# Layer norms of the first rows among the last attention products, shared row pools, and a start with eight adjacency loads

## The chip, the cores and the metric

The kernel runs on one core of one Trainium2 chip. A core has five engines that run side by side: TensorE (PE) for matrix products and transposes, VectorE (DVE), ScalarE (ACT), GpSimd (POOL), and SyncE (SP), which here only issues DMAs. Operands lie in SBUF, products land in PSUM. The metric is the device time of one launch in microseconds.

## The reference

The input is 4096 rows `x` of 256 features and a 4096 x 4096 adjacency of 0 and 1 with about 0.8% of ones and a full diagonal. Two graph attention layers come first, then one transformer layer:

```python
# twice: graph attention, 8 heads of 32 features
Wh = einsum('nd,hdo->hno', x, W)
e = leaky_relu(src[:, :, None] + dst[:, None, :], 0.2)     # src, dst = Wh . a
alpha = softmax(where(adj > 0, e, -9e15))
x = elu(einsum('hnm,hmo->nho', alpha, Wh)) + x
# once: transformer
q, k, v = split(layer_norm(x, g1, be1) @ w_qkv)
attn = softmax(where(adj != 0, q k^T * 32**-0.5, -inf))
x = x + (attn v) @ w_proj + b_proj
out = x + gelu(layer_norm(x, g2, be2) @ w1 + b1) @ w2 + b2
```

## The kernel before

**The two attention layers** are in `graph_attention`. The exponential of the leaky ReLU of a sum is one of two products of exponentials, depending on the sign of the sum. So the kernel needs per head only a 0/1 matrix that says where there is an edge and the sum is positive, the adjacency itself for all heads, and two sets of values weighted with exponentials. Sums over tokens are then products of 0/1 tiles with values, in f16 parts.

The work is cut into 256 *groups*: layer `l` (2), block `nb` of output rows (4 of 1024 rows), head pair `p` (4), and group `g` of four token tiles (8). Each group is 128 places of four products on PE (L1302), about 6 us. Beside its products every group carries a list `side` of steps for other engines, spread by a share of the group (`beside(steps, since, until)`). The steps are:

- `compare(i + 2)`: the 0/1 tile of the group after next. ACT makes one part of it (L1066), DVE another (L1068); one DVE instruction then puts the adjacency mask on (L1073). The comparison takes `s_b`, a broadcast of the terms of the rows, loaded through DRAM (`s_d`).
- `mask_load` (L855), `mask_clip` (L864, DVE: adjacency to fp8) and `mask_turn` (L886 PE transposes, L888 ACT copies): the adjacency, turned. The mask is kept in DRAM for the later head pairs, blocks and layers. The loads go into three `g_adj` buffers, the clips into six `adj_8` buffers.
- `preparation(l, q, bank)`: for one group `q` of four token tiles, the features are transposed (L961, L964), multiplied with the weights (L974), and the terms copied out (L981, DVE). ACT takes three exponentials of them (L987, L988), DVE the largest value (L989), the product of values and exponentials (L995, L1001). `split` makes two f16 halves: ACT casts the first (L1006), POOL subtracts (L1007). `term_rows` turns the terms (L1012, L1016) and stores them (L1019). Layer 1 has its first two preparations in `begin`, and six beside the first groups; layer 2 has eight beside the last groups of layer 1.
- `take`: a step of `pair_end` (L1101 to L1142), which closes a block and head pair on DVE, ACT and POOL, from copies of the PSUM banks that ACT makes (L1308, L1314).

The order on PE, ACT and DVE in `graph_attention` is that of the program text (a manual schedule over these three engines, which ends with the function). SP's order, and that of all engines in the transformer's first phase, is made by the scheduler.

`begin` loads the first rows and weights and three adjacency tiles, runs the preparations of `q` = 0 and 1, turns the first eight adjacency units (a unit is two row tiles of 1024 columns), and makes the comparisons of the first two groups.

**The transformer** (`unshifted_transformer`) opens with its QKV phase over eight blocks of 512 rows. `ready` loads the rows of a block and normalises them (`normed`: L1401 and L1402 mean, L1406 squares, L1410 root, L1414 normalised rows). `turned` transposes (L1430, PE) and copies with gamma and beta (L1433, ACT). Then come the products for k and q (L1502, copies L1506 ff) and v (L1521, L1528). Attention follows (L1554 to L1651), with the denominators' way over DRAM (`den_d` L1601, `u_dens` L1604, inverse L1608, L1609, `u_wide` L1614). The tail loads the weights (L1667 to L1679), and `projected` loads rows and attention (L742, L1692), projects (L1699, L1706) and normalises; the feed-forward follows (L1721, L1728, L1737, L1744, out L1745).

`Checks` collects conditions under which the fast path holds; otherwise a general path runs at the end.

Of the kernel before, what the change touches and what calls it, by code (L numbers as in the profile page):

```python
# [22 lines left out]
P = 128  # L23
# [727 lines left out]
def graph_attention(  # L751
# [6 lines left out]
    checks: Checks,  # L758
):

# [36 lines left out]
    stage_p = ctx.enter_context(tc.tile_pool(name="g_stage", bufs=2))  # L797
    rows_p = ctx.enter_context(tc.tile_pool(name="g_rows", bufs=2))
    t_p = ctx.enter_context(tc.tile_pool(name="g_t", bufs=3))
    s_p = ctx.enter_context(tc.tile_pool(name="g_s", bufs=2))  # L800
# [5 lines left out]
    ident_f = keep.tile([P, P], F32, name="g_ident_f")  # L806
    make_identity(nc, ident_f)
# [43 lines left out]
    def mask_load(nb, c, i):  # L851

        r = rows_p.tile([P, 2, G * P], I32, name="g_adj", bufs=3)
        at = STARTS[0][nb] * P + i * 2 * P
        nc.sync.dma_start(  # L855
            r,
            adj[at : at + 2 * P, c * G * P : (c + 1) * G * P].rearrange("(k r) m -> k r m", r=2),
        )
        loaded[nb, c, i] = r

    def mask_clip(nb, c, i):

        v = rows_p.tile([P, G * P, 2], F8, name="adj_8", bufs=6)
# [86 lines left out]
    def preparation(l, q, bank):  # L950
# [19 lines left out]
        def values(t):  # L970
# [10 lines left out]
            nc.vector.tensor_copy(  # L981
# [3 lines left out]
            big = some.tile([P, 2, H], F32, name="g_big")  # L985
            for i, scale in enumerate((-1.0, -LRELU)):
                nc.scalar.activation(big[:, i, :], L.negd[:, at, :], AF.Exp, scale=scale)  # L987
            nc.scalar.activation(L.r[:, at, :], L.terms[:, 0, at, :], AF.Exp, scale=LRELU - 1.0)  # L988
# [4 lines left out]
            prod = held[t] = some.tile([P, H, 2, V1], F32, name="g_prod")  # L993
# [9 lines left out]
        def split(t):  # L1003
            part = held.pop(t).rearrange("p h i v -> p h (i v)")
            halves = vst[q][:, t].rearrange("p h (k v) -> p h k v", k=2)
            nc.scalar.copy(halves[:, :, 0, :], part)  # L1006
            nc.gpsimd.tensor_tensor(halves[:, :, 1, :], part, halves[:, :, 0, :], op=ALU.subtract)  # L1007

        def term_rows():
# [5 lines left out]
            sr = some.tile([G * H, P], F32, name="g_sr")  # L1015
# [186 lines left out]
    def begin():  # L1202
# [3 lines left out]
        load_ahead(3)  # L1206
        units = own[: 2 * 2 * NW]
        for q in range(2):
            for k, step in enumerate(preparation(0, q, spare_bank)):
                step()  # L1210
                if q == 1 and k in (2, 4, 6, 8):
                    mask_clip(*units[k // 2 - 1])
        s_of[0, 0, 0] = s_fetch(0, 0, 0)
        for k, u in enumerate(units):
            mask_turn(*u)
            if k + 4 < len(units):
                mask_clip(*units[k + 4])
            else:
                mask_clip(*turns[0][k + 4 - len(units)])
# [8 lines left out]
    for i, (l, nb, p, g) in enumerate(groups):  # L1228
# [15 lines left out]
        if made:  # L1244
            steps = preparation(*made, lambda: turn_bank([P, 512], F32))
            beside(steps, 0.0, 0.9)
        if i + 2 < len(groups):
            steps = compare(i + 2)
            beside(steps[:-1], 0.25 if made else 0.0, 0.95)
            beside(steps[-1:], 0.96, 1.0)  # L1250
        beside([lambda u=u: mask_turn(*u) for u in turns.get(i, ())], 0.0, 0.9)
# [76 lines left out]

@with_exitstack
def unshifted_transformer(  # L1330
    ctx: ExitStack,
    tc: tile.TileContext,
    rows,
    mask_d,
    w_qkv: bass.AP,
# [3 lines left out]
    b1: bass.AP,  # L1339
    w2: bass.AP,  # L1340
    b2: bass.AP,
    g1: bass.AP,
    be1: bass.AP,
    g2: bass.AP,
    be2: bass.AP,
    out: bass.AP,
    checks: Checks,
):
# [30 lines left out]
    def by_feature(src, n, name):  # L1379
        t = wts.tile([P, n], F32, name=name)  # L1380
        with nc.allow_non_contiguous_dma(reason="one small vector"):
            nc.sync.dma_start(t, src.rearrange("(c p) -> p c", p=P))
        return t

    g1_sb = by_feature(g1, DC, "u_g1")
    be1_sb = by_feature(be1, DC, "u_be1")
    g2_sb = by_feature(g2, DC, "u_g2")
    be2_sb = by_feature(be2, DC, "u_be2")
    b1_sb = by_feature(b1, FC, "u_b1")
    ones = wts.tile([P, O], F32, name="u_ones")  # L1390
    nc.vector.memset(ones, 1.0)
    eps = wts.tile([P, 1], F32, name="u_eps")
    nc.vector.memset(eps, LN_EPS)
    ident_f = wts.tile([P, P], F32, name="u_ident")
    make_identity(nc, ident_f)
    dens = wts.tile([P, NQ, QI], F32, name="u_dens")

    def normed(xs, ln):

# [432 lines left out]
```

## Time and profile before

Three runs: 3472.72 to 3482.42 us, median 3479.99. The profiled execution has a span of 3480.2 us, with a mean granted PE clock of 0.983.

| stage | from to us | PE busy us | DVE busy us | ACT busy us |
|---|---|---|---|---|
| first loads and preparations | 0 to 62 | 19.05 | 31.73 | 24.56 |
| groups with preparation, layer 1 | 62 to 160 | 77.56 | 80.16 | 66.72 |
| groups, adjacency still loading | 160 to 380 | 211.32 | 210.31 | 198.26 |
| groups with preparation, layer 2 (part) | 880 to 985 | 86.10 | 83.98 | 74.49 |
| groups of layer 2 | 1034 to 1699 | 661.50 | 607.76 | 586.15 |
| its last eight groups | 1699 to 1746 | 46.69 | 36.23 | 34.44 |
| last pair, first norms | 1746 to 1763 | 4.73 | 13.24 | 12.74 |
| most of the QKV phase | 1763 to 1870 | 95.24 | 37.40 | 53.40 |
| end of attention, first projection | 3183 to 3220 | 15.49 | 8.87 | 7.30 |
| feed-forward | 3220 to 3480 | 251.50 | 42.15 | 85.70 |

Busy time is the time in which the engine works on an instruction; it may be less than the stage's length because the engine waits. A stage whose PE column equals its length is bound by PE. The stages of `graph_attention` have three busy engines and one order for each, so a wait in one soon becomes a wait in another.

### The profile page before, as it was taken

The page shows a single profiled execution, that of the slowest core. Times are in us where ns is not written, and L with a number is a line of the kernel's source. Part 1 is how long each engine was busy: PE and PEld are TensorE (multiplying, and loading weights), DVE is VectorE, ACT ScalarE, POOL GpSimd, SP SyncE. Part 2 cuts the span into 40 slices and gives each one's busy share as a digit, 9 for nine tenths or more (in the row PEclk, how much of TensorE's full clock was granted, in tenths as well). Part 3 has the DMA queues.
Part 4 walks back from the last instruction along what each step waited for, and adds up shares of the span by engine and source line. Part 5 has one row for each costly group of instructions (what it writes and reads, how often), then busy time and mean ns, then how long its engine had stood idle before and what let it go on. Part 6 is the DMA issues. An engine that isn't in the chain of part 4 may idle for free.

```text
span 3480.2 us, 97728 instructions
## 1 busy us (share of the span) xinstructions
PE 3297.8 (95%) x43156; PEld 2098.1 (60%) x43156; DVE 2880.6 (83%) x3250; ACT 2655.5 (76%) x3381; POOL 1323.4 (38%) x602
## 2 busy tenths in 40 slices
PE   4899999999889999999988999999999999997999
PEld 3799999999789999999953111111111111112666
DVE  6899999999779999999945999999999999996111
ACT  4799899988778888888855777777777777775332
POOL 1300000000210000000003999999999999996110
PEclk7999999999999999999989999999999999998999
DMA  6666555421311212121064010101011010002110
GB/s 203 190 181 205 154 154 164 139 84 27 96 51 39 72 48 87 39 75 39 12 178 113 19 31 19 32 25 25 25 26 37 13 44 10 26 10 67 44 47 26
DMA packets 214721, 250.57 MB, mean 72 GB/s; under 512 B 88528, under 2 KB 135632, under 8 KB 214288
## 3 DMA queue, kind: packets, MB, share of 16 engines
q1 hardware_dynamic: 214288, 244.25, 23.6%
q8 instruction: 339, 5.55, 0.7%
q14 instruction: 94, 0.77, 0.1%
HBM read 201.73 MB, written 42.47 MB: 70 GB/s over the span
## 4 chain that ended last, share of the span: by engine, by line
PE 39%; DVE 7%; ACT 4%; POOL 2%; issue 1%; DMA 1%; SPq 0%; DVEq 0%; ACTq 0%; POOLq 0%
PE u_ps L1554 12%; PE u_av L1568 11%; PE u_dn L1568 6%; DVE u_e L1563 4%; PE misc L1737 3%; PE bank L1302 2%; POOL u_both L1651 2%; PE misc L1502 2%; ACT u_ps L1561 1%; PE misc L1721 1%; PE misc L1521 1%; ACT ln_square L1406 1%; PE misc L1430 1%; DVE t L1073 1%; ACT t L1066 1%
## 5 line engine op out<-in xcount | busy, mean ns | idle before, releaser
L1302 PE MATMUL bank<-vst,t 128*128 128x66 f16 (+1 forms) x24576 | 1524.2, 203 | 47.5 <-DVE t L1073 39.6
L1302 PEld LDWEIGHTS <-t 128*128 128x128 fp8e4 x24576 | 1506.1, 97 | 66.5 <-DVE t L1073 47.9
L1302 PE MATMUL bank<-vst,mask 128*128 128x132 f16 x8192 | 1506.3, 222 | 0.0
L1066 ACT ACTIVATE t<-s_b,g_terms 128x1024 int8<-128x1024 f32 x1151 | 1243.6, 1165 | 98.6 <-PE bank L1302 94.7
L1651 POOL TENSOR_TENSOR u_both<-u_e 128x1024 f32<-128x1024 f32 x512 | 1200.1, 2368 | 232.6 <-DMA u_k<-half_d 126.1
L1563 DVE SCALAR_TENSOR_TENSOR u_e<-u_mask,u_ps 128x1024 f32<-128x1024 uint8 x1024 | 1201.7, 1215 | 89.2 <-ACT u_ps L1561 84.1
L1561 ACT ACTIVATE u_ps<-u_ps 128x1024 f32<-128x1024 f32 x1024 | 1010.8, 1008 | 281.4 <-PE u_ps L1554 262.4
L1302 PEld LDWEIGHTS <-mask 128*128 128x128 fp8e4 x8192 | 803.4, 98 | 0.0
L1073 DVE TENSOR_TENSOR t<-t,mask 128x2048 int32<-128x2048 int32 x256 | 589.8, 2304 | 111.0 <-ACT t L1066 89.6
L1068 DVE TENSOR_SCALAR t<-s_b,g_terms 128x1024 fp8e4<-128x1024 f32 x897 | 636.2, 753 | 0.0
L1554 PE MATMUL u_ps<-u_q,u_k 128*128 128x512 f16 x2048 | 579.1, 384 | 17.8 <-DVE u_e L1563 17.2
L1554 PEld LDWEIGHTS <-u_k 128*128 128x128 f16 x2048 | 139.0, 97 | 723.6 <-issue 664.6
L1568 PE MATMUL u_av<-u_e,u_v 128*32 128x512 f32 x4096 | 547.2, 606 | 0.0
L1007 POOL TENSOR_TENSOR vst<-g_prod,vst 128x528 f16<-128x528 f32 x64 | 83.9, 1321 | 938.5 <-ACT vst L1006 915.6
masks.py:197 POOL MEMSET u_ident<- 128x128 f32 x1 | 0.2, 205 | 727.5 <-ACT ln_square L1406 727.5
L1568 PE MATMUL u_dn<-u_both,u_ones 128*32 128x512 f32 x2048 | 274.0, 605 | 1.3 <-POOL u_both L1651 1.3
L1568 PEld LDWEIGHTS u_av<-u_e,u_v 128*32 128x32 f32 x4096 | 81.0, 108 | 219.2 <-issue 210.5
L1728 ACT ACTIVATE u_hid<-misc,u_b 128x512 f32<-128x512 f32 x64 | 42.3, 683 | 142.6 <-PE misc L1721 142.5
L1744 DVE TENSOR_TENSOR u_xres<-u_xres,misc 128x256 f32<-128x256 f32 x32 | 13.5, 421 | 122.7 <-PE misc L1737 122.7
L1737 PE MATMUL misc<-u_w,u_hid 128*128 128x256 f32 x512 | 111.8, 379 | 0.0
L1721 PE MATMUL misc<-ln_cols,u_w 128*128 128x512 f32 x256 | 111.2, 592 | 0.0
L864 DVE TENSOR_SCALAR adj<-g_adj 128x1024 fp8e4<-128x1024 int32 x128 | 97.1, 760 | 15.7 <-DMA g_adj<-in_adj_dram 15.7
(120 smaller groups left out, 1633.2 us busy)
## 6 DMA issues: line engine op xcount, KB each, us to landing
g_adj<-in_adj_dram SPq DMA_DIRECT2D x128, 512.0 KB
mask<-mask SPq DMA_DIRECT2D x128, 256.0 KB
s_b<-s_d SPq DMA_DIRECT2D x64, 512.0 KB
u_mask<-mask SPq DMA_DIRECT2D x32, 512.0 KB
mask<-stage SPq DMA_DIRECT2D x48, 256.0 KB
rows<-e_x SPq DMA_DIRECT2D x32, 256.0 KB
half_d<-u_halves SPq DMA_DIRECT2D x32, 256.0 KB
u_k<-half_d SPq DMA_DIRECT2D x32, 256.0 KB
```

The lines of the kernel that those rows point to most:

```text
L864: nc.vector.tensor_scalar(v.rearrange("p m r -> p r m"), loaded.pop((nb, c, i)), 1.0, -(2.0**-30), op0=ALU.min, op1=ALU.max, saturate=False,)
L1066: nc.scalar.activation(to.bitcast(I8), s, AF.Sign, bias=negd, scale=-1.0)
L1068: nc.vector.tensor_scalar(to, s, negd, None, op0=ALU.is_ge, saturate=False)
L1073: nc.vector.tensor_tensor(both, both, m32.unsqueeze(1).to_broadcast(list(both.shape)), op=ALU.bitwise_and)
L1302: nc.tensor.matmul(to, left, right, start=k not in opened, stop=last)
L1554: nc.tensor.matmul(ps[:, j, :], k_st[:, h, mt * P : (mt + 1) * P], q_st[:, h, :], start=True, stop=True,)
L1561: nc.scalar.activation(ps, ps, AF.Exp, scale=SCALE)
L1563: nc.vector.scalar_tensor_tensor(e, mask, 0.0, ps, op0=ALU.not_equal, op1=ALU.mult)
L1568: nc.tensor.matmul(to[j * O : (j + 1) * O, :], lefts[j], es[j // 2][:, j % 2, :], start=start, stop=stop,)
L1651: nc.gpsimd.tensor_tensor(both, es_of[i - 1][u], es_of[i][u], op=ALU.add)
L1721: nc.tensor.matmul(ph, w1_sb[:, k, f * P : (f + 1) * P], hn[:, k, :], start=(k == 0), stop=(k == DC - 1),)
L1737: nc.tensor.matmul(po[:, :D], hid[:, f, at : at + P], w2_sb[:, f, :], start=(f == 0), stop=(f == FC - 1),)
```

## The change

1. **Norms.** `normed` and `turned` become methods of a class `Norms`, made at the kernel's start with the small vectors (five small loads, now first on SP's queue), one f32 identity and a pool of small tiles. A class `Ahead` holds the rows, weights and columns of the QKV phase in buffers of the attention layers: `w_qkv` in `g_adj` slots, rows in `g_rows` slots, columns in `g_ft` slots. Its `steps` for row blocks 0 and 1 are handed into the last eight groups of layer 2: loads in group 0, means in 1, squares in 2, both roots in 3, normalised rows in 5 and 6, transposes and copies of block 0 in 7. The weights' loads have no wait on the groups; SP's order has them right after the last adjacency load. In the QKV phase each iteration turns the next block, normalises the one after, and loads the one after that at its end.
2. **Pools.** `stage_p` and `rows_p` are made outside of both functions, at the other side of SBUF (`side="right"`), and closed after the QKV phase. `adj_8` has five buffers instead of six, `g_sr` one, `g_big` four.
3. **Start.** The first eight adjacency loads are issued at once, three into `g_adj`, four into "mask" slots and one into a "t8" slot. Four clips stand beside the first preparation, turns and four more clips beside the second.
4. **Preparation.** The terms' copy goes from DVE to ACT, the exponentials read PSUM directly, layer 1's products lie in one wide tile (`ev_broad`'s slot), and the first half of `split` goes from ACT to DVE, except in `begin`. `check_values` (three reductions and three comparisons), which nothing called before, is called once per layer.
5. **Tail.** The projection's weight is loaded again there, and rows and attention of block 0 are loaded ahead of `b2`, `w1` and `w2`.

```diff
-        v = rows_p.tile([P, G * P, 2], F8, name="adj_8", bufs=6)
+        v = rows_p.tile([P, G * P, 2], F8, name="adj_8", bufs=5)
...
-            nc.vector.tensor_copy(
+            nc.scalar.copy(
                 L.terms[:, :, at, :], pv[:, D : D + 2 * H].rearrange("p (k h) -> p k h", k=2)
             )
-            big = some.tile([P, 2, H], F32, name="g_big")
+            big = some.tile([P, 2, H], F32, name="g_big", bufs=4)
             for i, scale in enumerate((-1.0, -LRELU)):
-                nc.scalar.activation(big[:, i, :], L.negd[:, at, :], AF.Exp, scale=scale)
-            nc.scalar.activation(L.r[:, at, :], L.terms[:, 0, at, :], AF.Exp, scale=LRELU - 1.0)
+                nc.scalar.activation(big[:, i, :], pv[:, D + H : D + 2 * H], AF.Exp, scale=scale)
+            nc.scalar.activation(L.r[:, at, :], pv[:, D : D + H], AF.Exp, scale=LRELU - 1.0)
...
-            prod = held[t] = some.tile([P, H, 2, V1], F32, name="g_prod")
+            if l == 0:
+                if t == 0:
+                    held["prods"] = ep.tile([P, G, H, 2, V1], F32, name="ev_broad")
+                prod = held[t] = held["prods"][:, t]
+            else:
+                prod = held[t] = some.tile([P, H, 2, V1], F32, name="g_prod")
...
-            nc.scalar.copy(halves[:, :, 0, :], part)
+            if first:
+                nc.scalar.copy(halves[:, :, 0, :], part)
+            else:
+                nc.vector.tensor_copy(halves[:, :, 0, :], part)
             nc.gpsimd.tensor_tensor(halves[:, :, 1, :], part, halves[:, :, 0, :], op=ALU.subtract)
...
-        load_ahead(3)
+
         units = own[: 2 * 2 * NW]
+        del coming[: len(units)]
+        for k, u in enumerate(units):
+            place = None
+            if 3 <= k < 7:
+                place = mask_p.tile([P, 2, G * P], I32, name="mask")
+            elif k == 7:
+                place = t_p.tile([P, 2, G * P], I32, name="t8")
+            mask_load(*u, place)
         for q in range(2):
-            for k, step in enumerate(preparation(0, q, spare_bank)):
+            for k, step in enumerate(preparation(0, q, spare_bank, True)):
                 step()
+                if q == 0 and k in (3, 5, 7, 9):
+                    mask_clip(*units[(k - 3) // 2])
                 if q == 1 and k in (2, 4, 6, 8):
-                    mask_clip(*units[k // 2 - 1])
+                    mask_turn(*units[k // 2 - 1])
+                    mask_clip(*units[k // 2 + 3])
         s_of[0, 0, 0] = s_fetch(0, 0, 0)
-        for k, u in enumerate(units):
-            mask_turn(*u)
-            if k + 4 < len(units):
-                mask_clip(*units[k + 4])
-            else:
-                mask_clip(*turns[0][k + 4 - len(units)])
+        for k in range(4, len(units)):
+            mask_turn(*units[k])
+            mask_clip(*turns[0][k - 4])
...
             steps = preparation(*made, lambda: turn_bank([P, 512], F32))
+            if made[1] == NG - 1:
+                steps.append(lambda: check_values(made[0]))
             beside(steps, 0.0, 0.9)
...
+        if i >= len(groups) - NG:
+            mine = [step for at, step in handed if at == g]
+            beside([lambda step=step: step(lambda: turn_bank([P, HB], F32)) for step in mine], 0.0, 0.9)
...
+    def steps(self):
...
+        all_ = [(0, self.weights)]
+        for at, step in ((0, self.load), (1, mean), (2, squares)):
+            all_ += [(at, lambda bank, nb=nb, step=step: step(nb)) for nb in range(2)]
+        all_.append((3, lambda bank: roots()))
+        all_ += [(5 + nb, lambda bank, nb=nb: self.normed(nb)) for nb in range(2)]
+        all_ += [(7, lambda bank, c=c: self.turned(0, c, bank())) for c in range(self.D // P)]
+        return all_
...
-            standing = {nb: ready(nb) for nb in range(2)}
-            across = turned(standing.pop(0), g1_sb, be1_sb, lnc, ps_q)
+            wq_sb = ahead.w
+            ahead.load(2)
             for nb in range(NNB):
                 cols = slice(nb * NB, (nb + 1) * NB)
-                hn = across
-                if nb + 2 < NNB:
-                    standing[nb + 2] = ready(nb + 2)
-                if nb + 1 < NNB:
-                    across = turned(standing.pop(nb + 1), g1_sb, be1_sb, lnc, ps_q)
+                hn = ahead.hn.pop(nb)
+                if nb + 1 < NNB:
+                    for c in range(DC):
+                        ahead.turned(nb + 1, c, ps_q.tile([P, NB], F32, name="misc"))
+                if nb + 2 < NNB:
+                    ahead.moments(nb + 2)
+                    ahead.normed(nb + 2)
...
                     nc.scalar.copy(v_sb[:, nb * TB + t, :], pv[:, :D])
+                if nb + 3 < NNB:
+                    ahead.load(nb + 3)
...
+        pools.close()
...
         bp_sb = by_row(b_proj, "u_bp")
-        b2_sb = by_row(b2, "u_b2")
-        w1_sb = big.tile([P, DC, F], F32, name="u_w1")
-        nc.sync.dma_start(w1_sb, w1.rearrange("(c p) f -> p c f", p=P))
-        w2_sb = big.tile([P, FC, D], F32, name="u_w2")
-        nc.sync.dma_start(w2_sb, w2.rearrange("(c p) e -> p c e", p=P))
+        wp_sb = big.tile([P, DC, D], F32, name="u_wp")
+        nc.sync.dma_start(wp_sb, w_proj.rearrange("(c p) e -> p c e", p=P))
...
+        first = rows_of(0)
+        b2_sb = by_row(b2, "u_b2")
+        w1_sb = big.tile([P, DC, F], F32, name="u_w1")
+        nc.sync.dma_start(w1_sb, w1.rearrange("(c p) f -> p c f", p=P))
+        w2_sb = big.tile([P, FC, D], F32, name="u_w2")
+        nc.sync.dma_start(w2_sb, w2.rearrange("(c p) e -> p c e", p=P))
...
+        stage_p = pools.enter_context(tc.tile_pool(name="g_stage", bufs=2, side="right"))
+        rows_p = pools.enter_context(tc.tile_pool(name="g_rows", bufs=2, side="right"))
+        ahead = Ahead(nc, norms, rows[2], stage_p, rows_p, w_qkv)
```

## The prediction, before the result was known

> **What bounds the kernel now.** I read the page first (busy time, slices, chain of waits), then busy time by stretch, then waits and timeline wherever TensorE falls below full.
>
> ```profile
> PE 3297.8 (95%) x43156; PEld 2098.1 (60%) x43156; DVE 2880.6 (83%) x3250; ACT 2655.5 (76%) x3381; POOL 1323.4 (38%) x602
> PE   4899999999889999999988999999999999997999
> PEclk7999999999999999999989999999999999998999
> ...
> PE 39%; DVE 7%; ACT 4%; POOL 2%; issue 1%; DMA 1%; SPq 0%; DVEq 0%; ACTq 0%; POOLq 0%
> ```
>
> TensorE is the bound: 182 us of 3480.2 are not PE. The slices show where a change can win: the first two (87 us each), the two eights at slices 11 and 12 (preparation of layer 2), the two at 21 and 22 (the passage from layer 2 to the transformer), and the 7 near the end. By stretch:
>
> ```profile
> 40.00:62.00 22.00, 0.61 (x4) 0.34 (x4) 8.76 (x11) 9.58 (x10) 0.00 (x0) 0.50 0.92 307
> 62.00:160.00 98.00, 77.56 (x1022) 66.70 (x1023) 80.16 (x149) 66.72 (x162) 30.42 (x23) 0.96 0.55 171
> ...
> 880.00:985.00 105.00, 86.10 (x1273) 76.15 (x1271) 83.98 (x158) 74.49 (x169) 31.07 (x24) 0.98 0.27 86
> 1034.00:1699.00 665.00, 661.50 (x14429) 657.33 (x14427) 607.76 (x690) 586.15 (x697) 0.00 (x0) 1.00 0.18 53
> 1699.00:1746.00 47.00, 46.69 (x1024) 46.39 (x1022) 36.23 (x41) 34.44 (x44) 0.00 (x0) 1.00 0.06 14
> 1746.00:1763.00 17.00, 4.73 (x22) 3.53 (x20) 13.24 (x31) 12.74 (x30) 0.61 (x2) 0.59 0.69 204
> ```
>
> Columns after the length: busy PE, weight loads, DVE, ACT, POOL, then clock, DMA share, GB/s. At 40 to 62 everything waits on DMA at 0.92; at 62 to 160 and 880 to 985 no engine is full (PE 79% and 82%, DVE 82% and 80%), so there the waits decide; the last eight groups of layer 2 (1699 to 1746) have a full PE with 10.8 us of DVE and 12.6 of ACT to spare; 1746 to 1763 is a PE hole.
>
> Waits from 62 to 160, then single places in the timeline (start, length, engine, line, idle before and its releaser):
>
> ```profile
> ACT g_big L987 <- DVE g_terms L981: 26.6, 24, 2.7
> PE turn L974 <- DVE g_prod L1001: 11.6, 12, 1.2
> DVE g_prod L995 <- POOL vst L1007: 4.6, 6, 0.8
> ```
> ```profile
> 55.93 0.70 DVE L864 TENSOR_SCALAR adj<-g_adj 128x1024 fp8e4<-128x1024 int32 x1 [2.23 <-DMA g_adj<-in_adj_dram]
> 1701.94 13.67 ACT L1066 ACTIVATE t<-s_b,g_terms 128x1024 int8<-128x1024 f32 x13
> 1754.80 2.09 PE L1430 MATMUL misc<-u_ident,ln_rows 128*128 128x128 f32 x8 [8.57 <-DVE ln_rows L1414]
> 1760.58 2.19 PE L1430 MATMUL misc<-u_ident,ln_rows 128*128 128x128 f32 x8 [3.69 <-DVE ln_rows L1414]
> 1812.29 2.19 PE L1430 MATMUL misc<-u_ident,ln_rows 128*128 128x128 f32 x8 [3.92 <-DVE ln_rows L1414]
> 3186.97 1.25 SPq L1601 DMA_DIRECT2D den_d<-u_den  x4
> 3192.99 0.35 SPq L1604 DMA_DIRECT2D u_dens<-den_d  x1
> 3193.86 0.51 SPq L1692 DMA_DIRECT2D u_att<-att_d  x1
> 3198.92 5.73 PE L1699 MATMUL misc<-u_wp,u_att 128*128 128x256 f32 x16 [12.94 <-DMA u_att<-att_d]
> ```
>
> **What the Trainium skill says.** "TensorE: Matmul & The Clock Gate", "What's actually happening": an idle window of about 3.4 us halves the array's clock. The trace agrees: eight transposes take 2.09 to 2.19 us after these idles and 1.04 in the stream, and the first block's QKV products 8.77 us against 7.03 later. So a hole of PE costs more than its length. "SBUF — State Buffer", "Who interferes with whom": VectorE and GpSimd share a port pair that one holds for a whole instruction. The trace agrees: a clip (L864) takes 0.69 us alone and 1.65 beside POOL's L1007. "VectorE: DVE Perf Modes", "Mode 2×_2P — use both read ports for one tensor": a one-source copy inside SBUF may run at two results per cycle. The trace has no such DVE copy here; L1139, one source, 512 elements of f32 in SBUF, takes 0.42 us and two-source L1140 0.69. I use those as the two ends for the new split copy.
>
> **Part 1, the start.** First products now begin at 62.3 us. The chain back: mask L1073 at 60.04 (2.29), five compares from 56.54, the clip at 55.93, which waited for an adjacency load; the clips waited 15.7 us in all on such loads, while the loads themselves were issued late, behind clips that free slots. The change issues eight loads (4.2 MB) at once from about 5.3 us, so at the measured 307 GB/s they are there by about 20 us. Against it: five small loads come first on SP (five issues of 0.45 us, +2.3), the second token group's rows are queued behind the 4.2 MB (arrival 20 to 25 us instead of before 19.3), so preparation q=1 ends near 35 instead of 33; and in SP's order three of the four s_d row stores stand behind loads that wait for clips of units 8 to 11, so the broadcast s_b is issued at about 43 (39.1 before) and lands at about 48.5 (47.40 before). Eight ACT compares then take 8.4 us beside DVE's, and the mask follows: first products at about 56. Gain 6, from 0 (s_b later than 54) to 10.
>
> **Part 2, the 14 preparation groups** (6 in layer 1, 8 in layer 2). Removed from DVE: four terms copies, 0.09 each start to start, 0.36 a group. Added: four split copies of 528, 0.42 to 0.70 each, 1.7 to 2.8 a group, perhaps more when POOL's subtract (1.15 to 1.4 us) holds the port. ACT loses four casts (0.62 each, 0.52 start to start) and gains four small copies of about 0.15: minus 1.5. The hop from DVE to ACT ahead of the exponentials (26.6 us over 24 tokens, 1.1 each) goes, as they read PSUM; in layer 1 the single wide tile removes L995's wait on POOL (4.6 us over 6 groups, 0.76 a group). PE's wait for L1001 (11.6 over 6 groups, 1.9 each) shortens by what of the hop lies on it. DVE now has 98.0 − 80.2 = 17.8 us to spare over these 6 groups, 3.0 each, so +1.3 to +2.4 fits, just. I take +0.5 us a group gained in layer 1 (3 in all; ends −5 and +9), and 0 in layer 2, where the two-buffer wait stays (ends −8 and +6). One `adj_8` buffer less costs nothing: each clip starts at least 3.68 us after the transposes of the unit five before it. The value checks, three reductions and three comparisons once per layer, come to about 1.2 us of DVE a layer by L1685, whose reduction of 256 elements takes 0.42; −1 in all (0 to −2.5).
>
> **Part 3, norms in the last eight groups.** Added to ACT: eight squares with their accumulator reads (0.63 each, 5.1), two root sets (0.5) with two table loads of 1.28, two copies of 0.6: 9.4 of 12.6 spare. To DVE: two means (1.24 + 0.16) and two sets of four normalisations (1.5): 5.8 of 10.8 spare. To PE: eight transposes, 1.04, in full. The spare time of ACT is not spread evenly: 13 compares stand back to back from 1701.94 to 1715.6, and squares fall in the third group; the masks lead PE by only 1.4 to 1.9 us. A stall of about 1.5 us there is likely (0 to 6). So layer 2's last product ends at about 1746.2 + 2.5. The DMAs: two row loads and nothing of w_qkv, which goes into adjacency slots right behind the last adjacency load in layer 1; the DMA share is 0.06 there, so they are hidden.
>
> **Part 4, the passage.** Now from 1746.2 to the first QKV product at 1762.56: 16.4 us. After: ev copies free the banks, PE does the eight transposes of block 1 (1.0; block 0's are in part 3) and goes on to the QKV products of block 0, with its columns and weights in place. Left are about 1.5 us. Gain 16.4 − 1.5 − 1.0 of the transposes + 1.4 of the clock (8.77 against 7.03, most of it) = 15.3; minus the 2.5 above: 12.8, say 12 (7 to 15). The last pair's finish on DVE (L1101 to L1141, about 10 us) runs beside QKV products now, ahead of block 2's norm, which PE needs only after the 14 us of two blocks.
>
> **Part 5, QKV phase.** The holes before the transposes of blocks 5, 6 and 7 (3.92 each plus a slow clock) come from squares that ACT reaches after the copies of its iteration. That order stands in the new text. The last ones move by a microsecond either way: 0 to −1; I take −1.
>
> **Part 6, the tail.** PE waits 12.94 us for `u_att`, whose issue stands behind den_d's landing (5.11 us, behind the w1 and w2 loads) and u_dens. After, the first att load is ahead of b2, w1 and w2, issued near 3188.7, landing 4.9 later at most; den_d lands about 2.5 us sooner without w1 and w2 ahead of it. L1699 can then start near 3193 to 3195 and its chain moves with it, but the division's own part at 3196 stays for later blocks. Gain 5 (2 to 7). A second wp load is 0.26 MB, hidden.
>
> **Sum.** 6 + 3 + 0 − 1 + 12 − 1 + 5 = 24. Against the profiled span of 3480.2, which is the median of the other runs (3479.99): **3456 us**.
>
> **Rivals.** About 0.3%, 10.4 us, is what a measurement of this kernel can tell from no change: under 3469.6 is faster, over 3490.4 slower.
> - A, the sum above, 3447 to 3465: 0.55.
> - B, the hop was the limit of the preparation groups: PE loses 98 − 77.6 = 20.4 us in layer 1's six and 18.9 over 105 in layer 2. If of the 3.4 a group of layer 1 that makes 1.4 comes back in all 14, it is 20 instead of 3: about 3439. For it: 26.6 us of ACT waiting; against: DVE gets fuller. 0.20.
> - C, given back: the start stands still because s_b, and not the adjacency, ends the wait last (6 lost), and ACT's crowded last groups stall PE by 6 instead of 1.5 (5 lost), preparation gains nothing (3): about 3470. For it: s_b is issued behind more. 0.19, two thirds of it inside 0.3%.
> - D, slower: DVE becomes the bound of the 14 groups. The place is the split copy against POOL's subtract of the token before: at 0.70 plus a wait of up to 1.15 each, four cost 7.4, less 0.36 and 3.0 spare: 4 us a group, 56 in all, less the 21 that the other parts give: about 3515. It decides from (21 + 10.4)/14 = 2.2 us a group. Against it: copies and subtracts follow each other by token in any case, and POOL is idle 70%. 0.06.
>
> That it doesn't do what it says is not likely: the transposes of block 0 stand among the products in PE's order.
>
> **Numbers.** Faster 0.55 + 0.20 + 0.06 = 0.81, same 0.13, slower 0.06. The range 3438 to 3474 leaves out D, the outer part of B and the edge of C; A alone is 3447 to 3465.
>
> **What would show it.** First products near 56; no wait of g_big on g_terms, and the period of preparation groups at 15.8 instead of 16.3; PE whole to 1749 and the first L1502-like product within 3 us of it; L1699's twin starting near 3194. Wrong it is if DVE's compares or masks become PE's releaser in the preparation groups, if PE stands in the last eight groups for over 5 us, or if s_b lands after 54.

## The result and the profile after

The changed kernel takes 3461.38 us (median of 4 runs, 3457.66 to 3466.94) against 3480.85 (3472.72 to 3482.42) of the kernel before: ratio 0.995, 95% interval 0.9929 to 0.9971, so 19.5 us less. Its profiled run is the slowest of the four (3466.94, span 3465.2); the profiled pair differs by 15.0 us.

The page of the changed kernel: busy time, two rows of the slices, the chain of waits by engine.

```profile
PE 3293.5 (95%) x43156; PEld 2098.3 (61%) x43156; DVE 2899.7 (84%) x3254; ACT 2629.4 (76%) x3391; POOL 1328.6 (38%) x600
PE   4899999999889999999988999999999999998999
PEclk8999999999999999999999999999999999998999
PE 40%; DVE 7%; ACT 3%; POOL 2%; DMA 1%; issue 1%; SPq 0%; DVEq 0%; ACTq 0%; POOLq 0%
```

The slices hide the change: PE gains a tenth in one slice near the end, and its clock one in the first slice and one where the layers hand over to the transformer; it is busy 4 us less for the same instructions. DVE gained 19 us of work, ACT lost 26. What tells is the start of each group's first product and of each stage's first one, in both traces. (A group is 32 places of four products, 128 in all, and not 128 places. "Groups 0 to 9" is the time from the first product of group 0 to that of group 9.)

| stretch | before us | after us | gain us | forecast us |
|---|---|---|---|---|
| start to group 0 | 62.39 | 60.15 | +2.2 | +6 |
| groups 0 to 9, layer 1's preparations | 116.73 | 108.89 | +7.8 | +3 |
| groups 120 to 136, layer 2's preparations | 165.74 | 169.32 | −3.6 | −1, the checks in it |
| group 168 | 5.84 | 9.43 | −3.6 | none |
| last eight groups | 47.12 | 51.60 | −4.5 | −2.5 |
| last product to first QKV product | 16.56 | 2.25 | +14.3 | +13.9 |
| first QKV product to first of attention | 109.18 | 112.19 | −3.0 | +0.4 (1.4 clock, −1) |
| last score product to first of the feed-forward | 40.48 | 35.83 | +4.7 | +5 |

The rest (groups between, attention, feed-forward) adds 0.7 and makes 15.0. Of layer 2's 3.6 us, 1.0 is in group 131, which varies between runs. By stretch of the changed kernel, with the columns of before (PE, weight loads, DVE, ACT, POOL, clock, DMA share, GB/s):

```profile
40.00:60.00 20.00, 0.00 (x0) 0.00 (x0) 6.40 (x7) 5.46 (x6) 0.00 (x0) 0.50 0.70 227
60.00:151.00 91.00, 76.51 (x1027) 65.29 (x1028) 85.13 (x148) 59.57 (x167) 31.75 (x23) 0.98 0.60 181
873.00:1028.00 155.00, 130.37 (x1937) 118.17 (x1935) 133.56 (x223) 91.06 (x230) 47.28 (x32) 0.93 0.24 74
1697.00:1749.00 52.00, 48.36 (x1004) 48.04 (x1001) 42.88 (x56) 42.57 (x68) 0.00 (x0) 0.97 0.09 23
```

In layer 1's preparations DVE is now busy 94% of the time and ACT 65% (82% and 68% before), and still it is shorter: the waits, not the busy time, had set it. Waits from 58 to 160 us:

```profile
ACT g_terms L984 <- PE turn L977: 26.5, 24, 1.8
PE turn L977 <- DVE ev_broad L1009: 6.0, 10, 0.7
```

ACT still waits 26 us, but for PE and no longer for DVE; PE's wait for the products fell from 11.6 to 6.0 us.

The start, in the timeline: the broadcast's first issue in the kernel before, then SP's issues, a clip and ACT's comparisons in the changed one:

```profile
39.14 0.82 SPq L1049 DMA_DIRECT2D s_b<-s_d  x2
37.52 7.32 SPq L858 DMA_DIRECT2D g_adj<-in_adj_dram  x4
44.90 1.16 SPq L1030 DMA_DIRECT2D s_d<-g_sr  x3
49.15 1.74 SPq L1060 DMA_DIRECT2D s_b<-s_d  x4
43.58 0.70 DVE L867 TENSOR_SCALAR adj<-g_adj 128x1024 fp8e4<-128x1024 int32 x1 [3.93 <-DMA g_adj<-in_adj_dram]
54.54 8.42 ACT L1077 ACTIVATE t<-s_b,g_terms 128x1024 int8<-128x1024 f32 x8 [15.32 <-DMA s_b<-s_d]
```

The first eight adjacency tiles are clipped by 36.9, but three of the four stores of the terms stand behind four later adjacency loads. The last of these needs a buffer that a clip frees at 44.28, and this clip itself stood 3.93 us for a tile. So the broadcast of the terms is issued at 49.15 instead of 39.14, and ACT waits 15.3 us for it.

The passage, one of the QKV phase's holes, and the tail:

```profile
1748.03 1.09 PE L1412 MATMUL misc<-ident,g_rows 128*128 128x128 f32 x8 [1.10 <-ACT ev_narrow L1338]
1748.95 7.03 PE L1579 MATMUL misc<-g_ft,g_adj 128*128 128x512 f32 x16
1800.23 2.18 PE L1412 MATMUL misc<-ident,g_rows 128*128 128x128 f32 x8 [7.20 <-DVE g_rows L1399]
3177.09 0.47 SPq L1768 DMA_DIRECT2D u_att<-att_d  x1
3181.12 6.56 PE L1779 MATMUL misc<-u_wp,u_att 128*128 128x256 f32 x16 [6.39 <-DMA u_att<-att_d]
3194.05 3.11 DVE L1399 TENSOR_SCALAR ln_rows<-u_xres,n_mean,n_dev 128x256 f32<-128x256 f32 x4
```

PE stands 1.10 us where it stood 8.57 and 3.69, and the products that follow take 7.03 us from the first block on, where the first block took 8.77. The hole before block 5 grew from 3.92 to 7.20. In the tail PE waits 6.39 us for `u_att` instead of 12.94; but the normalisation that follows takes 3.11 us instead of 1.38.

### The profile page after: what moved, and what is told of

The parts are those of the page before. It is cut to its first block, busy times and chain, and to the rows that moved or that the text cites. A ratio compares the mean times of both kernels' runs of the same rounds, so it can differ in the third digit from the quotient of the medians.

```text
span 3465.2 us, 97706 instructions
## 1 busy us (share of the span) xinstructions
PE 3293.5 (95%) x43156; PEld 2098.3 (61%) x43156; DVE 2899.7 (84%) x3254; ACT 2629.4 (76%) x3391; POOL 1328.6 (38%) x600
## 4 chain that ended last, share of the span: by engine, by line
PE 40%; DVE 7%; ACT 3%; POOL 2%; DMA 1%; issue 1%; SPq 0%; DVEq 0%; ACTq 0%; POOLq 0%
PE u_ps L1634 12%; PE u_av L1648 12%; PE u_dn L1648 6%; DVE u_e L1643 4%; PE misc L1831 3%; PE bank L1326 3%; PE misc L1579 2%; POOL u_both L1731 1%; ACT u_ps L1641 1%; PE misc L1815 1%; PE misc L1598 1%; DMA u_xres<-rows 1%; PE misc L1412 1%; ACT t L1077 1%; DVE t L1084 1%
## 5 line engine op out<-in xcount | busy, mean ns | idle before, releaser
L1018 POOL TENSOR_TENSOR vst<-g_prod,vst 128x528 f16<-128x528 f32 x32 | 47.3, 1487 | 814.1 <-DVE vst L1017 807.7
L1822 ACT ACTIVATE u_hid<-misc,n_b 128x512 f32<-128x512 f32 x64 | 42.3, 683 | 142.5 <-PE misc L1815 142.4
L1648 PEld LDWEIGHTS u_dn<-u_both,u_ones 128*32 128x32 f32 x2048 | 40.6, 108 | 110.9 <-issue 108.4
L1332 ACT COPY ev_broad<-bank 128x396 f32<-128x396 f32 x192 | 89.4, 473 | 23.4 <-PE bank L1326 19.9
```

The costliest lines, as they stand in the source:

```text
L1332: nc.scalar.copy(ev[0][:, a:b].rearrange("p s v -> p (s v)"), acc[k][:, : (b - a) * 2 * VW],)
L1648: nc.tensor.matmul(to[j * O : (j + 1) * O, :], lefts[j], es[j // 2][:, j % 2, :], start=start, stop=stop,)
```

## The experiments

Each is the changed kernel with one edit, and is read from one profile, by stage. Whole times tell little here: each of these kernels but c1 and c2 ran once, and all but two (x9 and x10) lie between 3455 and 3468 us, where the changed kernel's own four runs spread over 9. Runs that don't touch a stage serve as its repeats. These stretches vary between runs of the same code: group 0's start (59.2 to 60.4), group 131 (11.9 to 15.9 us, it waits for a row load of layer 2; left out below), group 168 (5.8 to 8.1 in the other runs), the QKV phase (111.1 to 113.8) and the tail (35.2 to 36.1). The preparation stages:

| kernel | groups 0 to 9 us | groups 120 to 136 without 131 us |
|---|---|---|
| before | 116.7 | 150.8 |
| changed | 108.9 | 153.4 |
| x1, cast on ACT | 109.0 | 147.5 |
| x2, terms by way of DVE | 113.3 | 156.1 |
| x3, two buffers in layer 1 | 115.0 | 153.5 |
| x10, three buffers in layer 2 | 108.8 | 144.7 |

**x1: the cast back on ACT.**

```diff
-            if first:
+            if True:
                 nc.scalar.copy(halves[:, :, 0, :], part)
```

> The changed kernel with one edit: the first half of every split is cast by ACT again (as before the change), in both layers; everything else stays changed. Stages are read from the profile by the start of the first product of a group, against the same groups of the changed kernel (group 0 at 60.2, group 6 at 150.4, group 120 at 862.0, group 136 at 1031.3 us). Theory (the DVE copies are what layer 2's preparation lost, and the direct exponentials what layer 1 won): groups 120 to 136 take about 165.7 us as in the kernel before, instead of 169.3, so 3.6 us less; groups 0 to 6 stay within 1.5 us of the changed kernel's 90.2. Rival (the relief of ACT is what layer 1 won): groups 0 to 6 take 94 to 97 us, near the 97.3 of before. Second rival (layer 2's loss comes from the exponentials in ACT's order and not from the copies): groups 120 to 136 stay at 169 us.

Layer 1 is the same to 0.1 us, so moving the cast won nothing there. Layer 2 falls by 5.9 us without group 131, below the kernel before: the cast on DVE is what layer 2 lost, and the other edits won 3.3 there. Of the 5.9, 3.6 lie at one place, in groups 133 and 134 at the end of the last preparation (15.26 us in the changed kernel, 11.63 in x1): there the last casts, and the value checks behind them, stand on DVE ahead of a mask. PE waits 1.92 us for this mask and then runs at a granted clock of 0.50 between 1020 and 1022 us.

**x2: the terms by way of DVE again.**

```diff
-            nc.scalar.copy(
+            nc.vector.tensor_copy(
                 L.terms[:, :, at, :], ...
-    nc.scalar.activation(big[:, i, :], pv[:, D + H : D + 2 * H], AF.Exp, scale=scale)
+    nc.scalar.activation(big[:, i, :], L.negd[:, at, :], AF.Exp, scale=scale)
```

> The changed kernel with one edit: the terms are copied by DVE again and the three exponentials read this copy, as before the change; the split stays on DVE, and layer 1's products stay in the wide tile. Theory (reading PSUM directly is what the preparations of layer 1 won; the cast on ACT has been shown to change nothing there): groups 0 to 9 take about 115 us instead of the changed kernel's 108.9 (before: 116.7), and layer 2's groups 120 to 136 about 172.8 instead of 169.3 (with the split on ACT they took 162.3, 3.5 less than before). Rival (the wide tile won it, by L995's wait on POOL): groups 0 to 9 stay within 1.5 us of 108.9.

4.4 us are lost in layer 1 and 2.7 in layer 2, so the hop by way of DVE costs. Direct exponentials are a part of layer 1's gain, not all of it: a loss of 6.1 had been expected.

**x3: two buffers in layer 1.**

```diff
-            if l == 0:
+            if l < 0:
                 if t == 0:
                     held["prods"] = ep.tile([P, G, H, 2, V1], F32, name="ev_broad")
```

> The changed kernel with one edit: layer 1's products go through two g_prod buffers again, as before the change and as in layer 2. Theory (DVE's wait on POOL is off the path as long as DVE is not full, and direct exponentials made the gain): groups 0 to 9 take 109 to 111 us (changed kernel 108.9, before 116.7). Rival (two buffers with the split on DVE are what made layer 2 slow: DVE stands 1 us before every third product until POOL's subtract frees the buffer): groups 0 to 9 take 114 us or more, since layer 1 then has the same chain as layer 2.

6.1 us are lost: the rival held. With the cast on DVE the wide tile is needed. The two edits together gave 7.8, and taking either away costs 4.4 or 6.1, so they don't add up. In x2 and x3 the first products also come 2.3 and 2.0 us earlier (57.9 and 58.2), since the clip at 43.58 comes earlier; so at group 9 they stand only 2.2 and 4.1 us behind the changed kernel. Their edits reach into the start, and whether they bring this about is open.

**x10: three buffers in layer 2.**

```diff
-                prod = held[t] = some.tile([P, H, 2, V1], F32, name="g_prod")
+                prod = held[t] = some.tile([P, H, 2, V1], F32, name="g_prod", bufs=3)
...
-        v = rows_p.tile([P, G * P, 2], F8, name="adj_8", bufs=5)
+        v = rows_p.tile([P, G * P, 2], F8, name="adj_8", bufs=4)
```

> The changed kernel with three g_prod buffers in layer 2 instead of two, paid for with four adj_8 buffers instead of five. Only layer 2's preparations are read from it: groups 120 to 136 without group 131, whose row load lands at varying times (12.5 to 17.5 us in the runs so far). They took 153.4 us in the changed kernel, 150.8 before, 147.5 with the cast on ACT. Theory A (two buffers and a cast on DVE make a chain: DVE's next product waits for POOL's subtract, which waits for DVE's cast): 148 to 150 us. Theory B (DVE is simply too full with four casts more): 152 to 154 us, with the wait on POOL gone all the same.

8.7 us are won, more than theory A expected, and 2.8 more than by the cast on ACT with two buffers. Theory B falls: DVE has room for the cast. The chain is seen in the changed kernel's layer 2, in DVE's timeline and in its waits (the third line is of the kernel before):

```profile
911.87 0.69 DVE L1003 TENSOR_TENSOR g_prod<-turn,g_big 128x512 f32<-128x512 f32 x1 [1.02 <-POOL vst L1018]
DVE g_prod L1003 <- POOL vst L1018: 12.5, 14, 1.0
DVE g_prod L995 <- POOL vst L1007: 10.9, 13, 1.0
```

DVE casts token tile t−1, POOL starts to subtract it, and DVE's product for t+1 needs the buffer that POOL is still reading: up to 1.02 us each time, 14 times, of an engine that is busy 86% of the stage. With three buffers this wait is no longer among the waits of the stage. But the kernel before had it almost as long, with the cast on ACT; x1 has 4.0 us of it, 7 times. So a part of the 8.7 us may have lain open before the change too: three buffers with the cast on ACT were not run.

**x4: the terms' stores first.**

```diff
-        load_ahead(1)
+        if more:
+            load_ahead(1)
...
-                    mask_clip(*units[k // 2 + 3])
+                    mask_clip(*units[k // 2 + 3], False)
         s_of[0, 0, 0] = s_fetch(0, 0, 0)
+        load_ahead(5)
```

> The changed kernel with one edit: the clips of units 3 to 7 in the start do not issue the next adjacency load each; the five loads are issued after the terms' stores and the first broadcast in program order. Theory (the first products wait for s_b, which is issued at 49.15 us because three stores of s_d stand on SP behind four adjacency loads that wait for clips): s_d stores are out by about 38, s_b is issued at about 41 and lands at about 48, first products at about 53.5 instead of 60.15, 6 to 7 us earlier. Rival A (the adjacency loads bound the start: 0.9 DMA share): s_b lands early but the masks of the next groups come late, and by group 6 the gain is under 2 us. Rival B (s_b's broadcast of 1 MB needs the DMA rings that the loads fill): s_b is issued early and lands after 52, first products after 57.

The broadcast's first half is issued at 40.41 and ACT starts at 49.64; the first products come at 55.25, 4.9 us earlier, where 6 to 7 had been expected. By group 9 only 2.3 us are left. The other half went into the first group; its stretch in x4, in the changed kernel and in c2 (see below), which has the same edit at the start:

```profile
55.25:73.50 18.25, 16.28 (x170) 14.02 (x171) 12.88 (x24) 10.79 (x30) 2.67 (x2) 0.75 0.33 103
60.15:75.80 15.65, 13.76 (x170) 11.80 (x171) 12.87 (x24) 10.79 (x30) 2.67 (x2) 0.89 0.38 118
53.52:69.38 15.86, 13.98 (x170) 12.02 (x171) 12.86 (x24) 10.79 (x30) 2.67 (x2) 0.87 0.39 122
```

The instructions are the same, DVE and ACT are busy as long, and in x4 PE is busy 2.5 us longer at a granted clock of 0.75 instead of 0.89. So it is PE's clock and not the adjacency that gave the gain back. This is no fixed price of an early start: c1 pays it again (18.3 us), but c2 starts at 53.52, keeps a clock of 0.87, and reaches group 9 5.6 us earlier than the changed kernel. What decides is open.

**x5: squares in the head pair before.**

```diff
-        if i >= len(groups) - NG:
-            mine = [step for at, step in handed if at == g]
+        if i >= len(groups) - 2 * NG:
+            mine = [step for at, step in handed if at == i - (len(groups) - NG)]
...
-        for at, step in ((0, self.load), (1, mean), (2, squares)):
...
+        for at, step in ((-8, self.load), (-5, mean), (-4, squares)):
```

> The changed kernel with one edit: loads, means and squares of row blocks 0 and 1 are handed into the last groups of the head pair before (loads in its group 0, means in 3 and 4, squares in 4 and 5); roots, normalised rows and transposes stay where they are. Theory (in the changed kernel the last eight groups lose 3.6 us between group 250 and group 252 because eight squares of 0.63 us on ACT push the comparisons, and the mask then comes late): groups 250 to 252 take 11.7 us again instead of 15.9, and what is lost in the last eight groups falls from 4.5 to about 1 us (eight transposes); the pair before has ACT waiting for PE in its later groups, so it loses under 0.5. Rival (the table loads of the roots are part of it): 1.3 us or more of the loss stays at groups 251 to 253. Second rival (the loss only moves to the pair before): groups 240 to 248 take over 49 us instead of 47.2.

Groups 250 and 251 take 12.28 us, as before the change (15.88 changed; my 11.7 was that of another pair of groups), the last eight 48.01 instead of 51.60. The pair before loses 0.8, more than the 0.5 allowed. Groups 252 to 254 stay at 17.46: the roots' table loads cost nothing. In the changed kernel the loss is one wait between 1700 and 1730 us, and the slow clock after it (0.70 granted from 1715 to 1717):

```profile
PE bank L1326 <- DVE t L1084: 2.5, 1, 2.5
```

**x6: nothing handed.**

```diff
-            tc, adj, rows, mask_d, weights, checks, stage_p, rows_p, ident, ahead.steps()
+            tc, adj, rows, mask_d, weights, checks, stage_p, rows_p, ident, []
...
+            for _, step in ahead.steps():
+                step(lambda: ps_q.tile([P, NB], F32, name="misc"))
             wq_sb = ahead.w
```

> The changed kernel with one edit: nothing is handed into the last eight groups; the same steps for row blocks 0 and 1 stand at the start of the QKV phase. It tells what the handed steps alone are worth. Theory: groups 250 to 252 take 12.3 us (15.9 in the changed kernel), the last product comes 4.5 us earlier within its layer; from it to the first QKV product about 16 us instead of 2.25, and the first block of QKV is 1.7 us slower because of the clock; the net is 11 to 12 us slower than the changed kernel, the first products of QKV block 1 as a mark. Rival (the passage is shorter anyway, since weights and rows lie in buffers that are free long before): from the last product to the first QKV product under 10 us, net under 5.

The rival held, in a way that neither had: from the last product to the first transposes it takes 1.32 us, and to the first QKV product 3.12 (2.25 in the changed kernel, with half of the transposes). The scheduler put the norms as early as their rows allow, into group 168, on ACT between the copies that PE waits for:

```profile
1219.97 0.51 ACT L1379 ACTIVATE adj<-g_rows,n_mean 128x256 f32<-128x256 f32 x1 [5.22 <-DVE n_mean L1372]
1221.11 0.22 PE L1326 MATMUL bank<-vst,t 128*128 128x66 f16 x2 [1.57 <-ACT ev_narrow L1338]
```

Group 168 takes 13.72 us there, 7.9 more than in the kernel before, against the 4.5 that the handed steps cost in the last groups. So the run is no clean undo of the part. It shows that with the new buffers the passage is short also where the scheduler places the norms, and its time, 3465.95, lies inside the spread of the changed kernel. What the whole part is worth, 14.3 less 4.5, rests on the two traces of before and after; what placing the steps by hand adds is not shown.

**x7 and x9: the QKV phase.** x7 loads the rows earlier:

```diff
                         ahead.turned(nb + 1, c, ps_q.tile([P, NB], F32, name="misc"))
+                if nb + 3 < NNB:
+                    ahead.load(nb + 3)
...
-                if nb + 3 < NNB:
-                    ahead.load(nb + 3)
```

> The changed kernel with one edit: in the QKV phase the rows of block nb+3 are loaded right after the transposes of block nb+1, which free their buffer, instead of at the end of the iteration. Theory (the scheduler puts the mean and squares of a block behind the copies of its iteration because it takes the rows to arrive late, and PE then stands before the transposes of blocks 5, 6 and 7, at a halved clock after it): squares come among the copies, the idle before the three sets of transposes (7.20, 3.92, 3.92 us) goes, and with it 1.1 us of slow transposes and 0.8 to 1.2 us of slow products each; the first product of attention comes 15 to 20 us earlier than the changed kernel's 1861.1. Rival (the order of ACT is the same or the rows do arrive late): idle of 3 us or more stays before each set, gain under 5 us.

The rival held: 111.1 us, no less than in some of the runs that leave the phase alone. The hole before block 5, 7.20 in all of those but x6, went to 4.60; those before 6 and 7 stayed near 3.9, since ACT reached the squares after the copies of v as ever. x9 has the earlier load too, and orders PE, ACT and DVE by hand from block 1 on, with each step placed after one cast and its subtraction:

```diff
+                if nb == 1:
+                    qkv.enter_context(tc.manual_schedule(engines=by_hand))
...
+                parts = ahead.parts(nb + 2) if nb + 2 < NNB else []
...
                             halves[:, 1, c, :], pq, halves[:, 0, c, :], op=ALU.subtract
                         )
+                        if parts:
+                            parts.pop(0)()
```

> The changed kernel with the QKV phase ordered by hand from its second block on (PE, ACT and DVE): rows of block nb+3 are loaded after the transposes of nb+1, the mean of nb+2 stands ahead of the block's products on DVE, its squares in two pairs after the first two casts on ACT, its root after the third, its normalised rows after the third subtraction, and the copies of v last. It follows the run with earlier loads alone, where three of the idles of PE stayed because ACT reached the squares after the copies of v. Theory (the place of the squares in ACT's order makes the idles): no idle over 1 us before the transposes of blocks 2 to 7, transposes 1.04 and products 7.03 us, so that each block takes 11.2 us and the first product of attention comes 18 to 21 us earlier after the first QKV product than the 112.2 us of the changed kernel (before the change: 109.2). Rival (ACT or the DMAs of the halves are too full for an earlier square: the phase shows a DMA share of 0.64): idles stay or move to the casts, under 8 us gained. Second rival: ordered by hand, the casts stand behind squares and PE waits for PSUM, blocks over 12 us.

88.4 us instead of 112.2, more than expected. PE has no hole in the phase before the attention's products. x7 shows that the earlier load alone does not do this; the fixed order and the place of the squares in it were not tried apart:

```profile
1785.94 1.04 PE L1412 MATMUL misc<-ident,g_rows 128*128 128x128 f32 x8
1786.81 7.03 PE L1603 MATMUL misc<-g_ft,g_adj 128*128 128x512 f32 x16
```

**x8: the tail's second rows early.**

```diff
-        first = rows_of(0)
+        first, second = rows_of(0), rows_of(1)
...
-                res_next, res_n = projected(*rows_of(nb + 1))
+                res_next, res_n = projected(*(rows_of(nb + 1) if nb else second))
```

> The changed kernel with one edit: rows and attention of block 1 of the tail are loaded right after those of block 0, ahead of b2, w1 and w2. Theory (in the changed kernel POOL's addition for block 1 falls on DVE's normalisation of block 0, which takes 3.11 us instead of 1.38, because the rows of block 1 land late; the two engines shut each other out): the addition runs by 3187, four normalisations take 1.4 us again, and from the last score product of attention to the first product of the feed-forward it takes 34.0 us instead of 35.7. Rival (w1 or the slow clock set the first product): 35 us or more, with the normalisation at 1.4 us all the same, or with w1 as PE's releaser.

```profile
3187.11 1.38 DVE L1399 TENSOR_SCALAR ln_rows<-u_xres,n_mean,n_dev 128x256 f32<-128x256 f32 x4
```

The normalisation is at 1.38 us with POOL's addition out of its way, and so it is in x1, where the tail is unchanged and the addition happened to end before it. So the two engines' overlap is what stretches it. What the edit is worth is less clear: the stage takes 34.84 us, the runs that leave the tail alone show 35.2 to 36.1, and c1 and c2, which have the edit, 33.5 and 35.7. Of the 1.7 us some 0.8 go again in x8, since the next 16 projection products take 5.60 us instead of 4.79.

**c1 and c2: the edits joined.** c1 has x4, x5, x8, x9 and the cast on ACT in layer 2; c2 has x10 in place of the cast.

> A kernel joined from the edits that won: cast on ACT in layer 2 only, terms' stores ahead of the adjacency loads, squares in the head pair before, the tail's second rows loaded early, and the QKV phase ordered by hand. The stages are independent, if the theory holds, so the gains add up: against the changed kernel's median of 3461.4 us 7 (layer 2) + 2.3 (start) + 2.8 (last groups) + 1 (tail) + 18 (QKV) = 31, so 3430 us, with a ratio to the kernel before near 0.985. Rival (gains in one stage are given back in a later one, as the start's 4.9 us were by half): over 3440 us.

> The joined kernel with one thing different: layer 2's split stays on DVE, with three g_prod buffers (and four adj_8 buffers), instead of the cast on ACT with two. Theory (the two-buffer chain is what the cast on DVE cost, and with three buffers DVE has room for it): groups 120 to 136 without group 131 take 144.7 us as in the run with three buffers alone, 2.6 less than the joined kernel's 147.3, and the median is near 3423 us against its 3425.9. Rival (with the start earlier, four adj_8 buffers hold back layer 1's clips): groups 0 to 9 take over 113 us (joined kernel 111.6), and the median is 3426 us or more.

c1 takes 3425.89 us (5 runs, 3425.37 to 3426.31), ratio to the kernel before 0.9839 (0.9825 to 0.9852). c2 takes 3420.94 (5 runs, 3417.73 to 3423.38), ratio 0.9822 (0.9809 to 0.9835). Both beat both kernels. Groups 120 to 136 without 131 take 147.3 and 142.5 us, and the QKV phase 88.4 in both: these stages' gains add up. In c2 groups 0 to 9 take 110.0 us (111.6 in c1), so four `adj_8` buffers hold nothing back there.

## Why the prediction was right, and where its steps were off

It came out: 3461.4 against 3456, inside both ranges, faster by more than 0.3%. That the sum fits is in part luck. The eight terms of the table were off by 20.9 us when the errors are added without their sign, and by 10.5 with it, and the profiled pair gained 15.0 us where the medians differ by 19.5. One of the prediction's own signs of being wrong also came: the second half of `s_b` was there only at 54.54, after the 54 that it had set.

- **Start, 6 forecast, 2.2 measured.** The step that failed is the time at which the broadcast `s_b` is issued: 43 in the prediction, 49.15 in the trace. That the stores stand behind the adjacency loads was seen; that these four loads hold SP's queue for 7.3 us, until a clip that waits for a tile, was not priced. It is rival C's mechanism, and x4 shows it. That a microsecond at the start is one in the total was taken for granted as well: 4.9 us earlier are worth 2.3 at group 9 in x4, and 6.6 are worth 5.6 in c2.
- **Layer 1's preparations, 3 forecast, 7.8 measured**, inside the stated ends of −5 and 9. The hop and the wait on POOL were both named; they were discounted because DVE would be nearly full. DVE at 94% proved harmless: without the cast on it the stage takes as long (x1), and the path ran through waits (x2, x3). This is rival B's mechanism, in layer 1 alone.
- **Layer 2's preparations, 0 and −1 for the checks forecast, −3.6 measured.** Rival D had the right place, the cast against POOL's subtract of the token before, but not the size: its price was 4 us a group and in all 14 groups. The measured cost of the cast is 5.9 us over eight groups. With a third buffer it goes (x10), so DVE's load alone is not the cause. "The two-buffer wait stays" was right for the wait itself, 10.9 us before and 12.5 after; the term that failed is the 0 put beside it, since with four casts more a group on DVE, and the same wait, a mask comes late (PE's 1.92 us). The checks show no cost of their own: in x1, which has them, the groups after the last preparation take 5.81 us. In the changed kernel they stand behind the last casts and ahead of the mask that PE waits for, and what share of that loss is theirs is open.
- **Last eight groups, −2.5 forecast, −4.5 measured.** The mechanism was as described: squares in the third group, a late mask. The stall was priced at 1.5 us and was 3.6 with the slow clock after it; block 0's transposes cost 0.9.
- **Passage, 13.9 and 1.4 for the clock forecast, 14.3 and 1.7 measured.** Right in each step that the two traces show.
- **QKV phase.** Leaving the clock out, −1 forecast, −4.7 measured. The missed term is the hole before block 5, 3.3 us longer because the mean also stands behind two casts and subtractions; another 2.0 us went before the first product of attention, of which 0.7 came back within it. These are of the profiled run; the phase varies by 2.7 us between runs of this code.
- **Tail, 5 forecast, 4.7 measured**, though by a different sum: `u_att` was there 6.5 us earlier and POOL's addition took 1.7 back.
- **Group 168, unforeseen, 3.6 us in the profiled run.** PE stood 1.90 us with nothing in the profile as releaser, and ran at a granted clock of 0.57 and 0.58 in the next 4 us.

```profile
1223.53 0.22 PE L1326 MATMUL bank<-vst,mask 128*128 128x132 f16 x1 [1.90 <-issue]
```

The same group takes 5.8 to 8.1 us in the other runs, x6 apart, and 5.84 in the kernel before. The profiled run is 5.6 us above its median, and this would be the larger part of it; the cause is open.

## What to carry to other kernels

When a copy moves between engines, look at the buffers of the chain it joins before the busy time of the engine it joins: here an engine at 94% was harmless in layer 1, and in layer 2 a third buffer won 8.7 us. A load made early helps only if what is queued behind it on the same DMA queue is not what ends the wait. And where a scheduler makes the order, the place of a short step in an engine's order can be worth more than the step: a block's mean, squares and normalised rows, put between its casts by hand together with an earlier load, took 24 us out of the QKV phase.

## What was not expected of the hardware

Four normalisations on DVE took 3.11 us beside one POOL addition of 2.34 us and 1.38 without it: the addition cost DVE three quarters of its own length. A DVE cast of 528 elements of f32 in SBUF to f16 took 0.42 us, the lower of the two ends that the prediction gave, and 1.39 us at most. An idle of 3.9 us on PE cost 2.0 to 2.6 us more in the clock: transposes at 2.15 to 2.19 instead of 1.04 us and the next 16 products at 7.83 to 8.51 instead of 7.03, over both kernels. An idle far shorter than the 3.4 us that the prediction cites was enough for a slow clock: it followed on idles of 1.90 us (group 168) and 1.92 us (group 134). After a table load of 1.28 us the next activation started at once (1718.71 to 1720.01 us).
